# A two-layer graph kernel: where the gathers and the work of the first neighbour list stand in the order of issue

## The chip, the cores and the metric

The kernel runs on one core of one Trainium2 chip. The metric is the device time of one execution in microseconds (us). For the kernel before, three runs are shown: 2752.2, 2752.31 and 2755.29, median 2752.31 us.

## The reference

The reference applies two graph attention layers, each with a residual sum and a layer norm, to `x` of shape (8, 2048, 256). A shared adjacency matrix `adj` (2048 x 2048, about 17 neighbours in a row on average, symmetric, with the diagonal) masks the attention.

```python
# layer 0
h1, h2, h3 = x @ W1, x @ W2, x @ W3
e = leaky_relu(h1 @ h2.T, 0.2);  e = where(adj > 0, e, -1e12)
x = layernorm(x + relu(softmax(e) @ h3))
# layer 1: 4 heads of 64
q = (x @ W).reshape(B, N, 4, 64)
e = leaky_relu(q @ a_src [:, :, None] + q @ a_dst [:, None]);  masked as above
x = layernorm(x + elu(softmax(e) @ q))
```

Every row attends only to its neighbours, so the kernel gathers rows by index instead of multiplying full matrices.

## The kernel before, in words

**Setup (up to line 336).** The adjacency matrix is loaded in sixteen blocks of 128 rows; in each, the non-zero entries are replaced by their column number plus one (`numbered`, line 244), the rows' degrees are counted, and the numbered block is written to a table `edges` in DRAM (line 250). The vertices are ranked by degree, and sixteen groups of 128 vertices are made, so that all rows of group t have at most SLOTS[t] neighbours: 38 in group 0, and 12, 13, 14, 15, 15 in groups 15, 14, 13, 12, 11. `order` holds the vertices of the groups. The first four batches of `x` are copied to a table `xg[0]` in DRAM (line 253), the other four to `xg[1]` later (line 928), both from the queue of SyncE (SP). The setup stands inside a manual schedule, which keeps its instructions in the source's order.

**Lists.** For each group a list of neighbours is made. `list_job` (line 471) gathers the group's 128 rows of 2048 numbers into a tile `nb`: for the first three groups that are worked on (15, 14, 13; the list `up` counts down) from `adj`, so that `numbered` is applied once more, for the others from `edges`. `neighbours` (line 479) then runs on VectorE (DVE): eight maxima at a time (`max`, line 488) and their removal (`match_replace`, line 491), in turn, until K neighbours are found, and three small instructions (lines 494 to 497) that write `idx`, the row numbers to gather.

**Units.** A unit is a layer, a half of the batch and a group: 32 units in layer 0 and 32 in layer 1. A unit of layer 0 does this:

- `before0` gathers the unit's own rows into `xo` (line 502 on), copies them on SP into a residual tile `xr` (line 509), transposes them on TensorE (PE, line 403), and multiplies by A = W1 W2^T to get `g`, which ScalarE (ACT) copies out of PSUM (line 520).
- `chunk_job` (line 451) gathers the neighbours' rows, two neighbours in a tile `s` of a ring of 16 tiles. Each gather is one indirect DMA from the queue of GpSimd (POOL, line 189), 128 rows of 4 KB.
- `logits0` multiplies each gathered row by `g` and sums (line 540, on DVE, four batches for each neighbour), then takes the softmax (lines 553 to 566, with the exponential on ACT, line 560).
- `sums0` scales the gathered rows by the softmax on ACT (line 631) and adds them up on PE by multiplying with the identity (line 609). When a tile's rows are added, its place in the ring is free for another gather.
- `after0` finishes the unit (residual, layer norm, projection to `q`) and writes rows for layer 1.

**What sets the order.** All this is written as Python generators. `tick` (line 891 on) calls `pump`, which issues the gathers whose list is ready and which have credit for a ring tile, then advances `logits`, and then up to two steps each of the queues `starts` (the `before` parts), `ends` (the `after` parts and `checks`) and `lists`. A list job and a chunk job each take one credit of 16; a list gives its credit back when it is ready. The calls so made give the source's order. POOL's instructions keep it through the whole kernel (line 337). The other engines' instructions are put in an order of their own by a scheduler when the kernel is built, except where a manual schedule is open.

`checks` (line 339) tests the degrees against SLOTS: a memset of a tile `worst` on POOL (line 342), a reduction into it on DVE (line 346), a transpose on PE (line 349) and two small instructions on DVE (lines 352, 353).

[...] The words "landing of a gather" mean the moment from which an instruction may use its data.

Of the kernel before, what the change touches and what calls it, by code (L numbers as in the profile page):

```python
# [123 lines left out]
def fast_path(  # L124
# [117 lines left out]
    def numbered(v):  # L242

        nc.vector.scalar_tensor_tensor(v, v.bitcast(I32), 0.0, count, ALU.is_gt, ALU.mult)
# [117 lines left out]
    up = list(range(NT))[::-1]  # L362
# [98 lines left out]
    def pump():  # L461
        while jobs and credits[0] > 0 and jobs[0][0]():
            credits[0] -= 1
            jobs.popleft()[1]()
# [13 lines left out]
    def neighbours(t):  # L478
        K, o = SLOTS[t], offs[t]
        while t not in loaded:  # L480
            yield
        v = loaded[t]
        if t in up[:3]:
            numbered(v)
        rounds = -(-K // 8)
        m = sp.tile([P, 40], F32, tag="m", name=f"m_{t}")
        for i in range(rounds):
            nc.vector.max(m[:, ts(i, 8)], v)  # L488
            yield
            if i + 1 < rounds:  # L490
                nc.vector.match_replace(v, m[:, ts(i, 8)], v, 0.0)
                yield
        credits[0] += 1
        nc.vector.tensor_scalar(neg[:, o : o + K], m[:, :K], 0.5, LOWEST, ALU.is_lt, ALU.mult)
        far = sp.tile([P, 40], F32, tag="far", name=f"far_{t}", bufs=2)[:, :K]
        nc.vector.tensor_scalar(far, m[:, :K], 0.5, FAR, ALU.is_lt, ALU.mult)
        nc.vector.scalar_tensor_tensor(
            idx[:, o : o + K], m[:, :K], 1.0, far, ALU.subtract, ALU.add
        )
        listed[t] = True  # L500
# [363 lines left out]
    for j, u in enumerate(units):  # L864
# [3 lines left out]
        elif j + 2 < NT:  # L868
            t = up[j + 2]
# [41 lines left out]
                    queue.popleft()  # L911
        clock[0] += 1

    for t in up[:3]:
        lists.append(neighbours(t))
    for u in units[:3]:
        starts.append(before[u.layer](u))
# [270 lines left out]
@with_exitstack  # L1188
def kernel(
    ctx: ExitStack,  # L1190
    tc: tile.TileContext,
    x: bass.AP,
    adj: bass.AP,
    w1: bass.AP,
    w2: bass.AP,
    w3: bass.AP,
    wq: bass.AP,
    a: bass.AP,
    out: bass.AP,
):  # L1200
    nc = tc.nc
    flagp = ctx.enter_context(tc.tile_pool(name="flag", bufs=1))
    flag = flagp.tile([1, 1], I32, tag="flag", name="flag")
    fast_path(tc, x, adj, w1, w2, w3, wq, a, out, flag)
    again = nc.values_load(
        flag, min_val=0, max_val=1, skip_runtime_bounds_check_because="a comparison gave it"
    )
    with tc.If(again > 0):
        general_path(tc, x, adj, w1, w2, w3, wq, a, out)
# [29 lines left out]
```

## Time and profile before

| what | us |
|---|---|
| median of three runs | 2752.31 |
| the profiled execution, its own time | 2757.27 |
| its span, from the first to the last instruction | 2755.5 |
| DVE busy | 2358.9 (86%) |
| PE busy | 1884.3 (68%) |
| POOL busy | 1509.5 (55%) |
| ACT busy | 1475.2 (54%) |
| DVE busy between 210 and 740 us | 510.4 of 530 |

Times of instructions are counted from the span's start. In rows of the timeline the first column is the start, the second the duration, then engine, source line, operation, what is written and read, shape and count; the bracket tells how long the engine had been idle before it and what ended that. The profiled execution is one execution; it took 5.0 us more than the median of the runs.

### The profile page before, as it was taken

What the parts mean: (1) busy time and instruction counts of PE and PEld (TensorE: products, weight loads), DVE (VectorE), ACT (ScalarE), POOL (GpSimd) and SP (SyncE); (2) the same over time, 40 slices, a digit from 0 to 9 for tenths busy, and PEclk for the clock granted to TensorE, in tenths of its full rate; (3) what the DMA queues carried; (4) which work ended last, traced back from release to release, by engine and by line L of the source; (5) the groups of instructions that cost most, each with busy time, mean ns of one, the idle gap of its engine ahead of it and who ended that gap; (6) DMA issues with size and microseconds to landing.
All of it is one profiled execution on the core that took longest, in us unless ns stands there. A gap on an engine that the chain in (4) does not pass through costs nothing. (4 is left out here: it accounts for less than half of the span.)

```text
span 2755.5 us, 41008 instructions
## 1 busy us (share of the span) xinstructions
PE 1884.3 (68%) x12003; PEld 788.4 (29%) x12003; DVE 2358.9 (86%) x7255; ACT 1475.2 (54%) x3465; POOL 1509.5 (55%) x1506
## 2 busy tenths in 40 slices
PE   0148888888776767676878677766566576675663
PEld 0123434333333334343333322311122112121221
DVE  7679999999987875777787786799999899999996
ACT  6137777878779986868788779221111111210212
POOL 1354454545444543544544455577767777775772
PEclk9569899999898888898888888878878888877886
DMA  9996776868674665767776765799789999986991
GB/s 388 386 374 216 263 278 226 281 227 274 233 244 168 212 218 197 262 215 254 234 263 229 257 223 193 272 337 351 270 313 352 329 335 335 361 312 254 340 337 66
DMA packets 248024, 749.41 MB, mean 272 GB/s; under 512 B 55712, under 2 KB 73248, under 8 KB 241648
## 3 DMA queue, kind: packets, MB, share of 16 engines
q0 software_dynamic: 192064, 644.32, 66.2%
q1 hardware_dynamic: 54464, 101.21, 10.3%
q8 instruction: 98, 1.61, 0.2%
q10 hardware_dynamic: 1264, 1.18, 0.1%
q14 instruction: 134, 1.10, 0.1%
HBM read 721.50 MB, written 84.48 MB: 292 GB/s over the span
## 5 line engine op out<-in xcount | busy, mean ns | idle before, releaser
L609 PE MATMUL acc<-s,ident 64*64 64x512 f32 x9632 | 1363.4, 659 | 448.5 <-issue 226.6
L540 DVE CUSTOM_DVE_ANT_0 j<-s,g 128x256 bf16<-128x256 f32 x2408 | 1019.5, 423 | 201.5 <-DMA s<-xg,idx 135.9
L189 POOL DMA_INDIRECT s<-xg,idx x602 | 631.0, 1048 | 769.0 <-ACT s L631 283.5
L631 ACT ACTIVATE s<-s,e 128x256 f32<-128x256 f32 x2408 | 999.2, 503 | 27.3 <-DVE e L566 26.5
L189 POOL DMA_INDIRECT s<-qg,idx x602 | 610.6, 1014 | 249.9 <-issue 123.8
L609 PEld LDWEIGHTS acc<-s,ident 64*64 64x64 f32 x9632 | 386.5, 145 | 1219.2 <-issue 675.6
L793 DVE TENSOR_TENSOR s<-s,p 128x2048 f32<-128x2048 f32 (+1 forms) x312 | 682.0, 2201 | 0.8 <-issue 0.2
L381 ACT ACTIVATE z<-mv,roots 128x4 f32<-128x4 f32 x64 | 18.9, 296 | 509.7 <-DVE mv L371 509.6
L540 DVE DVE_READ_ACCUMULATOR2_ANT e<- 128x1 f32 x2408 | 196.0, 81 | 0.0
L693 PE MATMUL ps_q<-wqs,x1T 128*128 128x264 f32 x512 | 147.4, 425 | 37.2 <-ACT x1T L405 25.9
L197 POOL DMA_INDIRECT out_dram<-o,oidx x128 | 129.9, 1015 | 75.2 <-ACT o L393 40.1
L403 PE MATMUL ps_t_x<-ident,xo 128*128 128x128 f32 x256 | 56.6, 364 | 165.1 <-DMA xo<-xg,order 165.1
L393 ACT ACTIVATE o<-xr,nmr,rstd 128x256 f32<-128x256 f32 x128 | 66.4, 589 | 134.1 <-DVE nmr L389 102.2
L413 PE MATMUL ps_p_g<-A,xT 128*128 128x256 f32 x512 | 129.8, 400 | 9.5 <-DVE so L702 5.5
L413 PE MATMUL ps_p_h<-w_sb,hT 128*128 128x256 f32 x512 | 127.8, 392 | 1.5 <-ACT hT L405 1.5
L693 PEld LDWEIGHTS ps_q<-wqs,x1T 128*128 128x128 f32 x512 | 100.5, 206 | 88.9 <-ACT x1T L405 31.2
L413 PEld LDWEIGHTS ps_p_g<-A,xT 128*128 128x128 f32 x512 | 97.1, 197 | 53.8 <-DVE so L702 9.0
L488 DVE MAX8 m<-nb 128x8 f32<-128x2048 f32 x44 | 100.5, 2285 | 13.3 <-DMA nb<-edges,order 13.2
L413 PEld LDWEIGHTS ps_p_h<-w_sb,hT 128*128 128x128 f32 x512 | 92.1, 190 | 63.3 <-issue 19.5
L760 ACT ACTIVATE e<-e 128x304 f32<-128x304 f32 (+11 forms) x34 | 14.9, 439 | 175.7 <-DVE e L759 175.6
L403 PEld LDWEIGHTS ps_t_x<-ident,xo 128*128 128x128 f32 x256 | 37.9, 184 | 232.9 <-issue 219.0
L393 ACT ACTIVATE y<-y,nmr,rstd 128x256 f32<-128x256 f32 x128 | 67.2, 589 | 32.1 <-DVE nmr L389 31.8
(128 smaller groups left out, 1426.6 us busy)
## 6 DMA issues: line engine op xcount, KB each, us to landing
adj<-in_adj_dram SPq DMA_DIRECT2D x16, 1024.0 KB, 8.9
edges<-adj SPq DMA_DIRECT2D x16, 1024.0 KB, 19.7
xr<-xo SPq DMA_DIRECT2D x128, 128.0 KB, 6.7
x1s<-y SPq DMA_DIRECT2D x32, 512.0 KB, 7.4
xr<-x1s SPq DMA_DIRECT2D x32, 512.0 KB, 6.9
s<-xg,idx POOLq DMA_INDIRECT x602
s<-qg,idx POOLq DMA_INDIRECT x602
xg<-in_x_dram SPq DMA_DIRECT2D x4, 2048.0 KB
```

The lines of the kernel that those rows point to most:

```text
L189: nc.gpsimd.indirect_dma_start(out=dst, out_offset=None, in_=table, in_offset=AT(ap=index, axis=0), bounds_check=table.shape[0] - 1, oob_i ...
L197: ins = nc.gpsimd.indirect_dma_start(out=table, out_offset=AT(ap=index, axis=0), in_=src, in_offset=None)
L381: nc.scalar.activation(z, mv[:, :, 1], AF.Ln, bias=w.roots[:, 0:1])
L393: nc.scalar.activation(dst[:, b, :], y[:, b, :], AF.Identity, bias=nmr[:, b : b + 1], scale=rstd[:, b : b + 1],)
L403: nc.tensor.transpose(pt[:, ts(j, P)], src[:, ts(4 * i + j, P)], ident)
L413: nc.tensor.matmul(pp[:, ts(j, C)], lhsT=srcT[:, ts((2 * i + j) * KC + k, P)], rhs=weight[:, k, :], start=(k == 0), stop=(k == KC - 1),)
L488: nc.vector.max(m[:, ts(i, 8)], v)
L540: nc.vector.tensor_tensor_reduce(out=jt, in0=rows[:, s, ts(b, C)], in1=u.g[:, ts(b, C)], scale=1.0, scalar=0.0, op0=ALU.mult, op1=ALU.add, ...
L609: nc.tensor.matmul(acc[r][64 * c : 64 * c + 64, :], lhsT=ident[rr, rr], rhs=rows[rr, s, c * 2 * w_ : (c + 1) * 2 * w_].rearrange("p (j w) ...
L631: nc.scalar.activation(v, v, AF.Copy, scale=u.p[i][:, b, k : k + 1])
L693: nc.tensor.matmul(pq[:, : C + 2 * H], lhsT=x1T[:, ts(i * KC + k, P)], rhs=w.wqs[:, k, :], start=(k == 0), stop=(k == KC - 1),)
L793: nc.vector.tensor_tensor(v, v, pv.unsqueeze(3).to_broadcast([P, n * HB, H, D]), ALU.mult)
```

## The change

Before the first tick, and inside a manual schedule for all engines, the change calls `pump` once and runs the whole generator of the first list (group 15). `pump` can issue only the three list gathers at that point, since no list is ready for a unit's gathers. The two other early lists (14 and 13) are queued as before.

```diff
-    for t in up[:3]:
+    with tc.manual_schedule():
+        pump()
+        for _ in neighbours(up[0]):
+            pass
+    for t in up[1:3]:
         lists.append(neighbours(t))
     for u in units[:3]:
         starts.append(before[u.layer](u))
```

Two things follow in the source's order. The first list is ready before the first tick, so the first tick's `pump` already issues all twelve gathers of unit 0, and the gather of the list of group 12, before `before0` of unit 0 gathers `xo` and before `checks` clears `worst`. And the other engines' schedules are made anew.

## The prediction

> **What bounds the kernel now.** I first read the page's busy slices, then the same sums by stage. The rows give the stretch, its length, and busy time with instruction counts of PE, PEld, DVE, ACT and POOL; then the granted clock, the DMA share and GB/s.
>
> ```profile
> 95.00:207.00 112.00, 40.78 (x199) 24.79 (x200) 81.94 (x233) 29.39 (x67) 53.89 (x52) 0.64 1.03 383
> 210.00:740.00 530.00, 444.64 (x2371) 198.60 (x2371) 510.39 (x2028) 417.51 (x1029) 249.63 (x238) 0.93 0.72 248
> 740.00:1800.00 1060.00, 783.20 (x4874) 363.66 (x4872) 809.54 (x3648) 816.19 (x2011) 512.43 (x492) 0.86 0.68 230
> ```
>
> Up to 207 us the DMA engines are full. From 187 to 740 us DVE is the bound (96%); what it waits for there is 3.3 us for `g` near 187 and under 2 us after 450. From 740 to 1800 us no engine is full: ring, gathers, products and scaling form a loop, and DVE waits 135.4 us for gathers. In all later stages each piece of work is released by the one before it, so a lag with which DVE enters its full stretch at 187 us reaches the end, unless the loop absorbs it.
>
> So the start decides. The timeline of DVE from 95 us, only the rows at which it had been idle and the last work before them:
>
> ```profile
> 106.91 2.29 DVE L244 SCALAR_TENSOR_TENSOR nb<-nb,count 128x2048 f32<-128x2048 int32 x1 [10.98 <-DMA nb<-in_adj_dram,order]
> ...
> 121.27 2.27 DVE L491 MATCH_REPLACE8 nb<-m,nb 128x2048 f32<-128x2048 f32 x1
> 123.46 0.15 DVE L497 SCALAR_TENSOR_TENSOR idx<-m,far 128x12 int32<-128x12 f32 x1
> ...
> 133.27 0.43 DVE L540 CUSTOM_DVE_ANT_0 j<-s,g 128x256 bf16<-128x256 f32 x1 [0.47 <-DMA s<-xg,idx]
> ...
> 152.46 2.29 DVE L488 MAX8 m<-nb 128x8 f32<-128x2048 f32 x1 [3.02 <-DMA nb<-edges,order]
> ...
> 177.79 2.29 DVE L488 MAX8 m<-nb 128x8 f32<-128x2048 f32 x1 [8.59 <-DMA nb<-edges,order]
> ...
> 187.42 0.42 DVE L540 CUSTOM_DVE_ANT_0 j<-s,g 128x256 bf16<-128x256 f32 x1 [2.62 <-ACT g L520]
> ```
>
> Unit 0's 48 products run from 133 to 167 us, in the shadow of full DMA engines; unit 1 begins at 187.42. The idle pieces 10.98, 0.31 (before the second list), 0.47, 3.02, 0.31 (for the exponential), 8.59, 2.62 and 0.71 sum to 27.0 us. On POOL:
>
> ```profile
> 99.41 0.99 POOL L189 DMA_INDIRECT xo<-xg,order  x1 [0.31 <-issue]
> 100.40 0.22 POOL L342 MEMSET worst<- 128x128 f32 x1
> 124.45 2.24 POOL L189 DMA_INDIRECT s<-xg,idx  x1 [23.83 <-DMA xg<-in_x_dram]
> ...
> 141.72 1.09 POOL L189 DMA_INDIRECT nb<-edges,order  x1 [0.31 <-issue]
> ```
>
> The row at 124.45 names a DMA, but `xo` reads the same table at 99.41; what it waited for is `idx` of group 15, written at 123.46. `xo` and `worst` were issued in that shadow.
>
> [...] share 1.03 from 95 to 207 us with POOL's gathers and SP's copies mixed, so moving a gather up or down there moves no total. [...] `xo` takes 0.99 us at 99.41, and its first transpose starts at 120.52.
>
> **The change part by part.** No instruction is added or removed; I compared the built programs. POOL's order differs only between its 83rd and 98th instructions, DVE's up to about 37%, ACT's to a third, PE's and SP's a little near the start; behind that they are equal.
>
> *The first list is not earlier, but later.* The manual schedule keeps the list's own instructions in order; other lists' are still put between them. Before `idx` of group 15 there stand seven instructions of 2048 columns in the kernel before and eight in the changed one (the second maximum of group 14 joins). One costs 2.2 us from start to start (116.60 to 118.86); the three small ones of `checks` that leave save 0.34. So `idx` moves from 123.46 to 125.3 and the first gather, 0.99 behind it, to 126.3: **+1.9 us**.
>
> *`xo` and `worst` go behind the gathers.* The new order on POOL is: twelve gathers of unit 0, the list gather of group 12, `xo`, `worst`. From the first gather to the list gather took 17.3 us (124.45 to 141.72): issue at 143.6. Issue to landing took 10.7 (141.72 to 152.46): the list lands at 154.3. `xo` follows 1.5 later; behind the next list gather, `xo` of unit 1 was issued 1.66 later and landed 1.7 later (177.79 and 179.52), so `xo` lands at 156.0, and `worst` is cleared at 146.4. The SP copies: all eight of line 928 now precede unit 0's `xr`; the DMA engines are full either way.
>
> *DVE behind it.* After the third list, at 134.9 (four more large instructions from 125.4, and small ones), stands the reduction into `worst`, held until 146.5, then the maxima of group 12, which wait for 154.3: **19.3 us idle**. The hold at 146.5 itself costs nothing, as the list lands later; without that cover it is 11.6. In the kernel before DVE did unit 0's products then. Now these follow the list's three large instructions (154.3 + 6.8 = 161.1), and wait for `g`. From landing to the ends of its two copies by ACT took 5.7 and 7.4 us (120.52 to 126.18 and 127.90): 161.7 and 163.4. Idle **0.6** and **0.7**. Then 46 products at 0.467 (137.32 to 137.79), 21.5 us, with group 11's list in between (6.8 and 0.3; landed by 181, so no wait): 192.0. Unit 1's `g` no longer stands behind unit 0's scalings on ACT: `xo` lands at 179.5 to 183, plus 5.7 is at most 189, so no wait.
>
> *The sum.* Idle of DVE: 11.3 + 19.3 + 0.6 + 0.7 + 0.3 = 32.2, against 27.0: **+5.2 us** on entering the full stretch. The check: unit 1 starts at 192.0 instead of 187.4, +4.6, with 1.2 of unit 0's softmax still to do, and with 0.35 of list work and a 0.71 wait saved, +4.7.
>
> *What is late next.* Unit 0's exponential now stands on ACT behind the copies of unit 2's transposed rows, whose gather waits for unit 0's `xr`; I get those copies at 186 to 197 us, and DVE wants the exponential at 195. That is a wait of 0 to 2 us, beyond that only if SP's copies are slower; I take **1.0**. Unit 0's scaling then starts at 196 instead of 169 and frees ring tiles later: tile 3 of unit 2 is gathered at about 202 and wanted at about 230, the list of group 10 lands by 221 and is wanted at 226. Hidden; its cover is 5 us for the list.
>
> *Reordered instructions from 200 to 740 us* do equal work on a full DVE. The trace cannot price them: a gain of at most the 2 us of waits left there, a loss of some 4; I take 0.
>
> Together **+6.2 us**: from the profiled span 2755.5 to 2761.7. The profiled execution's own time (2757.27) stands 5.0 above the median of the runs; on the median the forecast is 2752.3 + 6.2 = **2758.5 us**.
>
> **The rivals.** *Absorbed, not slower.* Between 740 and 1800 us DVE is idle 250 us of 1060. If ACT's scalings pace the loop there and had room at its entry, DVE's lag goes into its 135.4 us of waits for gathers. It decides once those waits shrink by 5 us. For it: ACT is 79% busy up to 740 and can catch up. Against: up to 740 ACT itself waits for DVE (42.4 us for `g` behind DVE's products, 22.2 for the exponential), so it carries the same lag. Time: 2752.3, at most 2755.
>
> *Stalls compound.* If `xr` of unit 0 lands 6 us later than I think, the exponential waits 5 us, and the list of group 10 loses its cover and waits 3: 2752.3 + 5.2 + 8 = 2765.5. For it: SP's wait for older copies took up to 16 us in this stretch. Against: the DMA engines' total is unchanged.
>
> *Faster.* If the first list came straight through, `idx` would be at 116.3, seven us earlier; the built order excludes it, so the change doesn't do what it says. A gain could then only come from the loop: a tenth less of 135.4 us, 13.5, less 5.2, gives 2744. Nothing in the profile speaks for it[...].
>
> **How the numbers follow.** The likeliest case (lag kept) has 0.55, its own range 2755 to 2762 (landing of list and `xo` each 2 us either way); the compound stall 0.15, the absorbed case 0.20, the faster one 0.10. A measurement of this kernel can tell about 0.2%, 5.5 us, from no change, so the line is 2757.8: of the likeliest case 0.38 lies above it and 0.17 within. Slower: 0.38 + 0.15 + 0.01 = 0.54; same: 0.17 + 0.19 = 0.36; faster 0.10. The range leaves out the faster case and a twentieth at each end: 2750 to 2767.
>
> **What would show it.** In the changed profile: the first gather of unit 0 near 126 us; a DVE idle of about 19 us ending at the list of group 12 near 154; unit 0's first product near 162; unit 1's near 192; DVE about 96% busy from there to 740; all marks behind 740 later by 5 to 7 us. I am wrong if unit 0's first product comes before 158 or after 166, if unit 1's does not lag, or if the lag at 740 is gone at 1800.

## The result: 13 us slower, twice what was forecast

The changed kernel takes 2768.15 us, median of 6 runs (2764.34 to 2772.86). The kernel before, run beside it, takes 2754.54 (6 runs, 2752.2 to 2758.37). The ratio is 1.0047 with a 95% interval of 1.0036 to 1.0058: 13 us slower, 10 to 16. The forecast was 2758.5, range 2750 to 2767. The direction was right; the time lies 1.2 us above the range.

The stages of the changed kernel, with the columns as before (stretch, length, busy time with counts of PE, PEld, DVE, ACT, POOL, granted clock, DMA share, GB/s):

```profile
95.00:207.00 112.00, 27.00 (x123) 18.89 (x123) 75.62 (x209) 15.15 (x34) 43.33 (x42) 0.58 0.95 343
210.00:740.00 530.00, 422.71 (x2408) 202.56 (x2408) 509.52 (x2014) 422.12 (x1043) 253.04 (x239) 0.89 0.74 251
740.00:1800.00 1060.00, 782.39 (x4920) 363.45 (x4912) 812.58 (x3676) 819.68 (x2020) 515.65 (x495) 0.87 0.69 232
```

The first row differs most. DVE is busy 75.6 us there instead of 81.9, and the DMA engines moved 343 GB/s instead of 383. They are full up to 185 us as before (share 1.04 from 95 to 185 us in both profiles); from 185 to 195 and from 195 to 207 us their share falls to 0.87 and 0.34 (1.03 and 0.96 before), so "the DMA engines are full either way" did not hold to the end of this stretch. From 210 to 740 us DVE is the bound as before, 96% busy. PE's granted clock is lower there (0.89 instead of 0.93); the experiments come back to that.

The timeline of DVE from 95 us, the rows at which it had been idle:

```profile
109.95 2.29 DVE L244 SCALAR_TENSOR_TENSOR nb<-nb,count 128x2048 f32<-128x2048 int32 x1 [12.29 <-DMA nb<-in_adj_dram,order]
...
148.67 0.18 DVE L346 TENSOR_REDUCE worst<-bad 128x1 f32<-128x32 f32 x1 [10.38 <-POOL worst L342]
157.67 2.30 DVE L488 MAX8 m<-nb 128x8 f32<-128x2048 f32 x1 [8.82 <-DMA nb<-edges,order]
...
165.34 0.42 DVE L540 CUSTOM_DVE_ANT_0 j<-s,g 128x256 bf16<-128x256 f32 x1 [0.60 <-ACT g L520]
...
167.06 0.43 DVE L540 CUSTOM_DVE_ANT_0 j<-s,g 128x256 bf16<-128x256 f32 x1 [0.69 <-ACT g L520]
```

And POOL's timeline, from the last list gather of the setup to the clearing of `worst`:

```profile
99.83 0.99 POOL L189 DMA_INDIRECT nb<-in_adj_dram,order  x1 [0.30 <-issue]
129.33 2.26 POOL L189 DMA_INDIRECT s<-xg,idx  x1 [28.52 <-issue]
...
146.13 0.99 POOL L189 DMA_INDIRECT nb<-edges,order  x1 [0.30 <-issue]
147.43 0.99 POOL L189 DMA_INDIRECT xo<-xg,order  x1 [0.30 <-issue]
148.42 0.22 POOL L342 MEMSET worst<- 128x128 f32 x1
```

The picture is the forecast one, piece by piece, 3.0 us later: group 15's list was numbered at 109.95 here and at 106.91 in the profile of before. On DVE nothing differs in order ahead of that row. From it to the first gather are 19.38 us (17.54 before): +1.84, where +1.9 was forecast. The hold at `worst` and the wait for group 12's list sum to 19.2 us (19.3 forecast), the two waits for `g` to 1.29 (1.3 forecast). Unit 1's first product stands at 195.1, forecast 192.0, which with the 3.0 is the same. That this fits to a tenth is in part luck: in the two later profiles of this order it stands 1.5 and 2.1 us later than forecast, counted from the first list in the same way.

So the steps hold in this profile, and yet the time is off by 9.65 us. The two profiled executions don't show why: their own times, 2765.93 and 2757.27, differ by 8.7 only. The experiments ask four things: how large the difference is in more runs; which of the moves makes it; whether a lag at the start reaches the end; and whether the later order of instructions (up to 740 us), which I had priced at 0, costs.

### The profile page after: what moved, and what is told of

It reads as the page before. It is cut to its first block, busy times and chain, and to the rows that moved or that the text cites. A ratio compares the mean times of both kernels' runs of the same rounds, so it can differ in the third digit from the quotient of the medians.

```text
span 2764.2 us, 40972 instructions
## 1 busy us (share of the span) xinstructions
PE 1858.3 (67%) x12003; PEld 787.9 (29%) x12003; DVE 2360.8 (85%) x7255; ACT 1473.0 (53%) x3465; POOL 1515.6 (55%) x1506
## 3 DMA queue, kind: packets, MB, share of 16 engines
q1 hardware_dynamic: 54464, 101.21, 10.3%
## 5 line engine op out<-in xcount | busy, mean ns | idle before, releaser
L609 PE MATMUL acc<-s,ident 64*64 64x512 f32 x9632 | 1328.5, 664 | 372.2 <-issue 220.0
L540 DVE CUSTOM_DVE_ANT_0 j<-s,g 128x256 bf16<-128x256 f32 x2408 | 1019.4, 423 | 193.0 <-DMA s<-xg,idx 129.1
L403 PE MATMUL ps_t_x<-ident,xo 128*128 128x128 f32 x256 | 57.7, 370 | 215.2 <-DMA xo<-xg,order 215.2
L405 ACT COPY xT<-ps_t_x 128x512 f32<-128x512 f32 x64 | 36.8, 577 | 152.6 <-PE ps_t_x L403 152.5
L760 ACT ACTIVATE e<-e 128x304 f32<-128x304 f32 (+11 forms) x34 | 14.9, 438 | 176.2 <-DVE e L759 176.1
## 6 DMA issues: line engine op xcount, KB each, us to landing
adj<-in_adj_dram SPq DMA_DIRECT2D x16, 1024.0 KB, 10.4
```

The source lines that it names most:

```text
L403: nc.tensor.transpose(pt[:, ts(j, P)], src[:, ts(4 * i + j, P)], ident)
L405: nc.scalar.copy(dst[:, ts(i, 512)], pt)
L540: nc.vector.tensor_tensor_reduce(out=jt, in0=rows[:, s, ts(b, C)], in1=u.g[:, ts(b, C)], scale=1.0, scalar=0.0, op0=ALU.mult, op1=ALU.add, ...
L609: nc.tensor.matmul(acc[r][64 * c : 64 * c + 64, :], lhsT=ident[rr, rr], rhs=rows[rr, s, c * 2 * w_ : (c + 1) * 2 * w_].rearrange("p (j w) ...
```

## The experiments

Three theories. **A**: the start makes DVE late, and that lag is kept. **B**: the rearranged instructions up to 740 us cost, whatever the start. **C**: the 3.0 us at the first list are a chance of one execution. The experiments ran in four sets; each set has its own runs of the kernel before on the same chip, and the differences below are against those (the ratio's interval times the time of before).

### Both kernels again

`before_again` and `before_3` are the kernel before, `after_again` and `after_3` the changed one. `own_last` reaches the changed order without a manual schedule: the ticks run the lists alone until the first one is ready. All five engines then have the changed kernel's order, so it counts as the changed kernel.

```diff
     for t in up[:3]:
         lists.append(neighbours(t))
+    while not listed[up[0]]:
+        tick(0)
+    pump()
     for u in units[:3]:
         starts.append(before[u.layer](u))
```

> The kernel before once more, for its spread and a second profile. Theory A (the changed kernel is slower because DVE enters its full stretch later, and that lag is kept) and theory B (it is slower because 1755 instructions of DVE and 807 of ACT stand in another order up to 740 us) both expect 0, within 2 us of the kernel before. Theory C (the 3.0 us by which the list of group 15 was numbered later in the changed profile, 109.95 against 106.91, is a chance of the one execution) expects this mark anywhere from 106 to 111 here; if the mark is set by the order of the instructions, it is within 0.5 of 106.9 again.

> The kernel before, without any manual schedule, but with the first ticks running the lists alone until the first one is ready, so that the twelve gathers are issued ahead of xo and worst. All five engines then have the changed kernel's order, instruction by instruction. Theory A and B: as the changed kernel, 10 to 16 us above the kernel before, with the group 12 list's maximum on DVE about 48 us behind the numbering of group 15's list (47.7 in the changed profile). Theory C: if the numbering is near 107 here, 3.0 us of the changed profile's lateness were chance, and unit 1's exponential stands near 218 rather than 221.

> The changed kernel once more, on one chip with the three others of this set, for a second profile and more runs. Theory A (lag of DVE at its entry, kept): 7 to 9 us above the kernel before, as the second kernel of this order came out (9 us), which means that 3 to 4 us of the first comparison's 13 were spread of the runs. Theory C would have the list of group 15 numbered between 106 and 108 here.

> The kernel before, profiled on the same chip as the three others of this set. Theories A and B: 0, within 2 us. In its profile the last list is ready about 618.9 us after the list of group 15 was numbered (618.8 and 619.0 in its two profiles so far), or more in proportion on a slower chip.

> The changed kernel, profiled on the same chip as the kernel before. Theory A: from the numbering of group 15's list to the last list 6 to 9 us more than in the profile of the kernel before of this set, of which DVE's idle time between the two marks explains all but 2, and the time 5 to 11 us above. Theory B: the idle time explains less than half of it.

| kernel | runs | median us | before beside it (runs) | difference us, interval |
|---|---|---|---|---|
| before_again | 14 | 2756.39 | 2757.44 (30) | -1.9, -4.4 to +0.6 |
| own_last | 6 | 2766.21 | 2757.44 (30) | +9.1, +5.8 to +12.4 |
| before_3 | 14 | 2755.49 | 2755.69 (44) | 0.0, -2.8 to +2.8 |
| after_3 | 11 | 2764.91 | 2755.69 (44) | +9.6, +6.6 to +13.0 |
| after_again | 22 | 2870.99 | 2864.77 (75) | +6.0, +2.9 to +9.2 |

The kernel before takes 2755.7 to 2757.4 in the larger samples, not 2752.3: the three runs shown were low ones. The change costs 9 us rather than 13. For `own_last` 10 to 16 us were expected, so its 9.1 fell a little short. The second set ran on a chip that takes 4% longer (2864.77 us for the kernel before); there the change costs 6.

The marks of the profiles, in us. "Numbered" is the start of the first L244 row of group 15's list, "unit 1" its first product, "list 11" and "last list" the writing of `idx` of group 11 and group 0, "last exp" the last exponential of layer 0; "idle" is DVE's idle time up to list 11, added up from the timeline's brackets.

| profile | numbered | unit 1 | list 11 | idle | last list | last exp | end |
|---|---|---|---|---|---|---|---|
| before | 106.9 | 187.4 | 188.3 | 55.6 | 725.7 | 1685.2 | 2755.5 |
| before_again | 106.0 | 187.5 | 188.3 | 55.6 | 725.0 | 1689.4 | 2760.4 |
| before_3 | 109.0 | 187.3 | 188.2 | 55.5 | 725.0 | 1684.5 | 2756.2 |
| changed | 109.9 | 195.1 | 194.4 | 64.1 | 735.7 | 1692.6 | 2764.2 |
| own_last | 106.5 | 193.7 | 193.0 | 62.8 | 734.2 | 1688.3 | 2760.9 |
| after_3 | 105.8 | 192.4 | 191.7 | 61.5 | 733.4 | 1687.9 | 2760.4 |

*C is right as far as it goes*: the first list is numbered anywhere from 105.8 to 110 in kernels of one order. But it explains little. In the kernel before, the entry to DVE's full stretch is at 187.3 to 187.5 whether the list was numbered at 106.0 or 109.0, and DVE's idle time up to list 11 is 55.5 or 55.6 in each. The later waits are shorter where the list is later: up to 450 us they sum to 16.6, 15.7 and 13.5 us with the list at 106.0, 106.9 and 109.0. In the changed kernel the entry moves with the first list in part (192.4 to 195.1).

The last list and the last exponential in a profile of either order, the kernel before first (`before_3`, `after_3`):

```profile
724.95 0.19 DVE L497 SCALAR_TENSOR_TENSOR idx<-m,far 128x38 int32<-128x38 f32 x1
1684.48 0.27 ACT L560 ACTIVATE e<-e 128x76 f32<-128x76 f32 x1 [2.89 <-DVE e L559]
```

```profile
733.38 0.19 DVE L497 SCALAR_TENSOR_TENSOR idx<-m,far 128x38 int32<-128x38 f32 x1
1687.88 0.27 ACT L560 ACTIVATE e<-e 128x76 f32<-128x76 f32 x1 [2.89 <-DVE e L559]
```

*B is not seen beyond a microsecond.* DVE's idle time between list 11 and the last list is 2.1 us on average before and 2.2 in the changed order. In the kernel before 0.7 of it is still the wait for unit 1's `g`; from 200 us on the two are 1.4 and 2.2, so the new order costs some 0.8 there. The last list is 9.2 later on average. Idle time up to it accounts for 7.4 of that (65.0 against 57.7), and 1.6 is that slightly more work stands ahead of it in the new order (busy time 648.2 against 646.6); that is moved work, no added work. So the lag proper is some 7.5 us. Counted from the numbering, as the expectation of `after_3` has it, the last list is 11.6 us later than in `before_3`, where 6 to 9 were expected; idle time explains 9.8 of that, and B would have had less than half.

*The clock* is a rival that none of the theories names. From 210 to 740 us PE's granted clock is 0.89 to 0.90 in the three profiles of the changed order and 0.93 to 0.94 in the three of the kernel before. DVE, the bound there, loses no more than the 0.8 us above. From 740 to 1690 us the clocks are 0.87 and 0.86, and `late_start` below is slower with 0.93 in the earlier stretch. So the lower clock isn't needed for the loss; why it is lower stays open.

### The list alone

`own_first`: the changed kernel, but `xo` and `worst` are issued before the first tick. POOL, ACT, PE and SP then have the order of the kernel before, and DVE differs in 28 instructions.

```diff
     ends.append(checks())
+    next(starts[0])
+    next(ends[0])
```

> The changed kernel, but with xo and worst issued ahead of the twelve gathers; the first list stays in its manual schedule. POOL, ACT, PE and SP then have exactly the order of the kernel before, and DVE differs from it in 28 instructions only (the 78th to the 106th); idx of group 15 has seven large instructions before it again. Theory A: first gather, first product (near 133 from a list numbered at 107) and unit 1's first product (near 187) as before, so 0, at most 2 us either way. If the manual schedule or the early first list costs something by itself: 5 us or more above the kernel before.

> The changed kernel with xo and worst ahead of the gathers (the list alone is changed), once more. Its time was that of the kernel before, but in its one profile the last list was ready at 732.4 us, 7 later than in the kernel before (725.0 to 725.7), after a 3.2 us wait for a list near 460. Theory A (the lag at the last list reaches the end): that was a chance of the one execution, so here the last list is ready within 3 us of 725, and the time is within 2.5 us of the kernel before. If the lag repeats at 7 while the time stays the same, a lag at this mark does not reach the end, and theory A falls.

Measured: 2756.57 us against 2757.44, -1.7 (-4.7 to +1.7, 14 runs), and 2754.42 against 2756.13, -1.1 (-3.6 to +1.7, 14 runs). So the manual schedule of the first list costs nothing that can be told, nor does it make that list earlier: `idx` of group 15 is written 16.5 us after the numbering, as in the kernel before (16.6). The place of `xo` and `worst` makes the whole difference. DVE's timeline of `own_first_2`, the main rows with idle time from the first product on:

```profile
136.96 0.43 DVE L540 CUSTOM_DVE_ANT_0 j<-s,g 128x256 bf16<-128x256 f32 x1 [4.82 <-DMA s<-xg,idx]
...
155.83 2.29 DVE L488 MAX8 m<-nb 128x8 f32<-128x2048 f32 x1 [0.54 <-DMA nb<-edges,order]
...
181.15 2.29 DVE L488 MAX8 m<-nb 128x8 f32<-128x2048 f32 x1 [8.51 <-DMA nb<-edges,order]
...
190.23 0.43 DVE L540 CUSTOM_DVE_ANT_0 j<-s,g 128x256 bf16<-128x256 f32 x1 [2.07 <-ACT g L520]
```

Unit 0's products begin at 137.0 again, ahead of the list of group 12, and the wait for that list is 0.5 us instead of 19. The last list is at 728.1, 3 late. Of the 7 in the first profile, 3.2 came of a wait for a list at 450 us, which isn't in the second: that part was a chance. Unit 1 enters at 189.8 and 190.2 in the two, 2.5 to 3 us late, and that did not show in the time; this is the first sign against a lag kept in full.

### The two halves

`worst_first` issues only `worst` ahead of the gathers (`next(ends[0])`), `xo_first` only `xo` (`next(starts[0])`).

> The changed kernel, but with worst cleared ahead of the twelve gathers; xo stays behind them. ACT, PE and SP keep the changed kernel's order, DVE differs in 38 instructions: the reduction into worst stands early, and seven instead of eight large instructions stand before idx of group 15. Theory A: the hold of 10.4 us at the reduction is covered by the landing of group 12's list, so it only turns into a longer wait for that list (19 minus 1.9 us in one piece); the first gather and all behind it come 1.9 us earlier than in the changed kernel: 8 to 14 us above the kernel before. If the hold itself is what costs: 10 us below the changed kernel, so 0 to 5 above the kernel before. Theory B: as the changed kernel.

> The changed kernel with worst cleared ahead of the gathers, once more. In its first profile DVE's idle time up to the list of group 11 was 58.9 us, against 62.8 and 64.1 in the two profiles of the changed order and 55.6 in the kernel before. Theory A: 3 to 6 us above the kernel before, and 3 to 5 below the changed kernel of this set. Theory B (the order of instructions up to 740 us costs, whatever the lag): no more than 1 us below the changed kernel.

> The changed kernel, but with xo issued ahead of the twelve gathers; worst stays behind them. SP then has the order of the kernel before; DVE still reduces into worst ahead of unit 0's products and waits there until about 147. Theory A: unit 0's products no longer wait for g (0.6 and 0.7 us), the rest stays: 1.3 us below the changed kernel. If it is xo's late issue that makes the changed kernel slow: within 2 us of the kernel before. Theory B: as the changed kernel.

> The changed kernel with only worst cleared ahead of the gathers. Theory A: last list ready near 730 (4.7 late, as in its first profile), the time 3 to 6 us above the kernel before. If the order of the instructions up to 740 us is what costs: 8 to 11 above, as the changed kernel.

> The changed kernel with only xo issued ahead of the gathers. Theory A: the last list 6 to 9 us late (on the other chip it was 1.2 before that of the changed kernel), the time 5 to 9 us above the kernel before. If xo's late issue is what costs: within 2 us of the kernel before.

| kernel | runs | median us | before (runs) | difference us, interval |
|---|---|---|---|---|
| worst_first | 9 | 2764.50 | 2757.44 (30) | +9.1, +6.1 to +12.4 |
| worst_first_2 | 22 | 2867.45 | 2864.77 (75) | +3.4, +0.6 to +6.0 |
| worst_first_3 | 5 | 2767.41 | 2756.13 (21) | +11.9, +8.3 to +15.4 |
| xo_first | 22 | 2867.76 | 2864.77 (75) | +3.2, -0.3 to +6.3 |
| xo_first_2 | 8 | 2763.07 | 2756.13 (21) | +6.9, +4.1 to +9.6 |

DVE's timeline of `worst_first_3`, where the reduction into `worst` is long done:

```profile
158.26 2.29 DVE L488 MAX8 m<-nb 128x8 f32<-128x2048 f32 x1 [18.73 <-DMA nb<-edges,order]
...
165.87 0.43 DVE L540 CUSTOM_DVE_ANT_0 j<-s,g 128x256 bf16<-128x256 f32 x1 [0.59 <-ACT g L520]
```

And of `xo_first_2`, where `g` is no longer waited for:

```profile
147.66 0.18 DVE L346 TENSOR_REDUCE worst<-bad 128x1 f32<-128x32 f32 x1 [11.34 <-POOL worst L342]
...
159.18 2.29 DVE L488 MAX8 m<-nb 128x8 f32<-128x2048 f32 x1 [10.31 <-DMA nb<-edges,order]
```

The hold at `worst`, 10 to 13 us, costs nothing by itself: without it DVE waits as long for the list behind it (18.7 in one piece), and the time stays at that of the changed kernel (+11.9 against +9.1 to +9.6). On the usual chips neither half gives back the 9 us. They are no sum of two costs: with either of the two behind the gathers the built order has the first maximum of group 12's list ahead of unit 0's products, and in `worst_first` `g` isn't there any sooner (DVE still waits 0.5 to 0.7 us for it). The products begin at 165.9 and 163.8, against 132 to 137 with both ahead; in `xo_first_2` the first of them shows no wait of its own and still comes behind the hold and the list's wait, 11.3 and 10.3 us. For `worst_first_3` theory A had expected a last list near 730 and 3 to 6 us, after the first profile of `worst_first` (729.9). Both missed: its last list is at 735.9 and its time 11.9 above, nearer to the 8 to 11 that the order up to 740 us was to cost. But the lag was there in full (last list 10.7 late); its size could not be read from the first profile alone. On the slower chip both halves came out between the two kernels, by less than their intervals can tell.

### A lag and nothing else

`late_start` is the kernel before with eight more maxima on DVE in the setup, ahead of the list gathers. POOL, ACT and PE keep the order of the kernel before, DVE but for the eight, SP but for six.

```diff
+    late8 = const.tile([P, 8], F32, tag="late8", name="late8")
+    for _ in range(8):
+        nc.vector.max(late8, keys)
     order = const.tile([P, NT], I32, tag="order", name="order")
```

> The kernel before with eight added maxima over 2048 columns on DVE in the setup, ahead of the list gathers: 8 x 2.25 = 18 us of delay there, and no other change: POOL, ACT and PE keep the order of the kernel before exactly, and DVE but for the eight; SP has six instructions moved. The copies of x run on meanwhile, so the waits for the lists of groups 12 and 11 (3.0 and 8.6 us) should shrink and take back some of it: the list of group 10 and the last list should be late by 7 to 18 us. Theory A (a lag at the entry is kept): the end is late by as much as the last list, within 3 us. The rival that the loop between 740 and 1800 us absorbs a lag: the end is late by less than half of that.

Measured: 2764.40 us (10 runs) against 2755.69, +11.3 (7.7 to 14.9). DVE's timeline (added lines shift the numbers by 3):

```profile
124.44 2.29 DVE L244 SCALAR_TENSOR_TENSOR nb<-nb,count 128x2048 f32<-128x2048 int32 x1 [9.53 <-DMA nb<-in_adj_dram,order]
...
183.84 2.29 DVE L491 MAX8 m<-nb 128x8 f32<-128x2048 f32 x1 [0.62 <-DMA nb<-edges,order]
...
198.22 0.42 DVE L543 CUSTOM_DVE_ANT_0 j<-s,g 128x256 bf16<-128x256 f32 x1 [7.37 <-ACT g L523]
```

The first list is 15.5 us later than in `before_3`, the waits for the lists of groups 12 and 11 shrink from 3.1 and 8.1 us to nothing and 0.6, and unit 1 enters at 198.2, 10.9 later, behind a wait for `g` of 7.4 us (1.0 in `before_3`). The last list comes 11.5 later. The time follows: a lag of 11.5 at that mark, with the order of before, costs about what the changed kernel's 9 cost. This is A for the runs, and it needs no B. The rival of a loop that takes up a lag by more than half falls for the runs (7.7 at least), but not for this kernel's profile, where the last exponential of layer 0 is only 5.1 late and the end 5.5.

The changed kernel's profiles say the same: +9.2 at the last list, +3.2 at the last exponential of layer 0 (means of three and three). The waits in question, DVE's for gathers between 740 and 1800 us (total, times, longest), of `before_3`:

```profile
DVE j L540 <- DMA s<-xg,idx: 133.6, 83, 6.6
```

and of `after_3`:

```profile
DVE j L540 <- DMA s<-xg,idx: 130.5, 84, 6.6
```

Over the three pairs of profiles they shrink by 5.1 us on average (134.9 to 129.8). So these profiles show the loop taking up more than half of the lag, with ends 4.5 us apart on average, while the medians are 9 apart. In the profiles of `worst_first_3` and `xo_first_2` less is taken up: the last list stands at 735.9 and 735.5, the last exponential at 1693.3 and 1692.6, the end at 2765.6 and 2764.7, against means of 725.2, 1686.4 and 2757.4 for the kernel before. How much the loop takes up in a usual execution stays open: ends of single profiles of one kernel differ by 5 us.

### All three lists in line

`straight`: `xo` and `worst` first, and then all three early lists one after the other in the manual schedule, so that no other list's instructions stand before `idx` of group 15. Against the changed kernel:

```diff
+    for u in units[:3]:
+        starts.append(before[u.layer](u))
+    ends.append(checks())
     with tc.manual_schedule():
         pump()
-        for _ in neighbours(up[0]):
-            pass
-    for t in up[1:3]:
-        lists.append(neighbours(t))
-    for u in units[:3]:
-        starts.append(before[u.layer](u))
-    ends.append(checks())
+        next(starts[0])
+        next(ends[0])
+        for t in up[:3]:
+            for _ in neighbours(t):
+                pass
```

> xo and worst first, and all three early lists run one after the other inside the manual schedule, so that only four large instructions stand before idx of group 15. Of the later order 1340 instructions of DVE and 566 of ACT are moved against the kernel before. First gather at about 117.5 instead of 124.5, list gather of group 12 at about 135. Theory A: DVE's waits between 133 and 155 (0.5 and 3.0 us) go, while the later wait for group 11's list may take some of it back as the DMA engines are full: 0 to 4 us below the kernel before. Theory B: the moved instructions cost, so that it comes out above the kernel before by 2 to 6 us.

> All three early lists one after the other in the manual schedule, xo and worst first, once more, now beside a profile of the kernel before on the same chip. It was 9.4 us faster than the kernel before in the last set, more than the 0 to 4 us expected. If it is the start alone: its last list is ready 7 to 12 us sooner after the numbering of group 15's list than in the kernel before (618.9), and the time is 6 to 12 us below. If the last result was a matter of that chip: 0 to 4 us below.

Measured: 2855.84 us (22 runs) against 2864.77 on the slower chip, -9.5 (-12.0 to -6.6), and 2751.20 (21 runs) against 2755.69, -5.8 (-8.3 to -3.0). It beats both kernels. The first was more than the 0 to 4 expected, the second a little less than the 6 to 12. DVE's timeline of `straight_2`:

```profile
106.45 2.29 DVE L244 SCALAR_TENSOR_TENSOR nb<-nb,count 128x2048 f32<-128x2048 int32 x1 [4.93 <-DMA nb<-in_adj_dram,order]
...
116.16 0.17 DVE L497 SCALAR_TENSOR_TENSOR idx<-m,far 128x12 int32<-128x12 f32 x1
126.39 0.42 DVE L540 CUSTOM_DVE_ANT_0 j<-s,g 128x256 bf16<-128x256 f32 x1 [5.52 <-DMA s<-xg,idx]
...
181.13 0.42 DVE L540 CUSTOM_DVE_ANT_0 j<-s,g 128x256 bf16<-128x256 f32 x1 [3.81 <-ACT g L520]
```

`idx` is written 9.7 us after the numbering (16.6 before), the first product comes 7 to 9 us earlier, and the two waits for lists are gone. Group 11's list is ready at 177.2 instead of 188.2, but DVE then waits 5.0 us for unit 1's `g`, which stands behind the list here, so unit 1 enters at 181.1, 6.2 earlier than in `before_3`. The last list is 5.5 earlier and the end of the profile 6.2. Again the difference at the last list is the difference in time, although 1340 instructions of DVE have moved; B had expected 2 to 6 us above.

## Why the forecast was wrong, step by step

The mechanism was right: DVE enters its full stretch late (192.4 to 195.1 us, not 187.3 to 187.5), because unit 0's products can no longer fill the wait for group 12's list (they begin at 162.4 to 165.3, not at 133.3 to 135.3). What failed are two terms of the sum, the base and the size of the lag.

**The base failed first.** "The profiled execution's own time (2757.27) stands 5.0 above the median of the runs; on the median the forecast is 2752.3 + 6.2." The median of three runs was taken as the kernel's time, and the profiled execution as slow. Over the 95 runs of the three sets on usual chips the medians are 2755.7 to 2757.4: the profiled execution was typical and the three runs were low. With a base of 2756.1 (the middle one of the three medians) the miss of 9.65 us divides into 3.8 of base, about 3.1 in the size of the change (6.2 forecast, 9.3 as the mean of `own_last` and `after_3`), and 2.7 by which the first six runs of the changed kernel were above 2756.1 + 9.3. The range had no term for the base at all.

**The sum, "+5.2 us on entering the full stretch", was short.** DVE's idle time up to 200 us, the second wait for `g` of the kernel before included, is 6.5 longer, three profiles against three. From the numbering on, the changed kernel's idle sum is 20.8, 22.9 and 22.3, mean 22.0 where 21.2 was forecast: group 12's list is had 47.7, 50.1 and 48.7 us after the numbering, forecast 47.4. That is 0.8. The other 0.5 are spread of the kernel before and of the setup, which a sum against one execution can't hold. Up to the last list 7.4 of idle time are seen, where 6.2 were forecast in all. The 1.9 from there to the 9.3 of the runs are not located in any profile; the intervals of the runs are wider than that.

**Unit 0's exponential, +1.0**, did not wait behind the copies of unit 2's transposed rows. ACT's row and DVE's next row in the first changed profile:

```profile
196.72 0.24 ACT L560 ACTIVATE e<-e 128x48 f32<-128x48 f32 x1 [4.00 <-DVE e L559]
197.00 0.20 DVE L563 TENSOR_REDUCE s<-e 128x4 f32<-128x48 f32 x1
```

ACT had waited 4.0 us for DVE itself, and DVE shows no wait for the exponential.

**The reordered instructions, 0**, came out at 0.8 us of idle time, within the stated bounds of -2 to +4.

**The list order (+1.9), the new order on POOL, the 19.3 us and the waits for `g`** came out to within half a microsecond in the changed profile. That the hold itself costs nothing is shown by `worst_first_3` (no hold, 18.7 us of wait for the list, +11.9). The forecast said what it cost "without that cover"; it did not say that either of the two late instructions alone is enough to keep unit 0's products out of the 19 us, which the halves show.

**The rivals.** "Compound stalls", 2765.5, was nearest in time and wrong in mechanism: of the lists after group 11's only that of group 10 is waited for up to 335 us, for 0.4 to 0.8 us, and unit 0's exponential not at all. "Absorbed" has something to it in the profiles: DVE waits 5.1 us less for gathers, and 5 was the amount at which the prediction said that it decides. But the runs are not within 2755. "Faster": the reading that a list in truth straight would be seven us earlier is shown by `straight_2` (9.7 us after the numbering, not 16.6), and the gain came from the start, not from the loop.

**The signs that it named.** In the first changed profile unit 0's first product stands at 165.3, inside the limit of 166, and unit 1's lags by 7.7. The last list is 10.0 late there and the last exponential still 7.4, so the lag isn't gone; in the means of three it falls from 9.2 to 3.2.

## What to carry to other kernels

Take the base from as many runs as the size of the change asks for, and give it a term in the range: here three runs were 4 us low, more than half of the effect forecast. The hold at `worst` (10.4 of 19.2 us) lay in a wait that was there anyway and cost nothing, but what stood behind it in order was the only work that could have filled that wait: ask what the engine would have done there, not only how long it waits. And the two late instructions, each of which left that work behind the list, did not add up; to undo the loss both had to be moved (-1.7 and -1.1 us, where either alone left +6.9 to +11.9 on the usual chips), and moving the list wholly into line, with both ahead of it, gained 5.8 us where the half measure lost 9.

## What the hardware showed that I had not expected

One of the chips took 2864.8 us for the kernel before (75 runs) where three sets on others took 2755.7 to 2757.4. Against the first profile of the changed kernel, its profile there is 17 us late at the last exponential of layer 0 (1709.9 against 1692.6) and 105 at the end (2869.5 against 2764.2), so most of it lies in layer 1. From 1800 to 2756 us PE is busy 754 us there for 4270 matmuls, against 612 for 4520, at a granted clock of 0.86 against 0.82: the granted clock isn't lower there, and the cause stays open. The signs of all differences were the same there.

In the kernel before a first list that is up to 3 us later does not delay the entry: it came at 106.0, 106.9 and 109.0 us and unit 1 at 187.5, 187.4 and 187.3. DVE waits for transfers and for `g` in between, and these waits took up the difference (up to 450 us they sum to 16.6, 15.7 and 13.5 us), while the DMA engines were full (share 1.03 from 95 to 207 us in the profile with 106.9).
